# Loading the per-batch conditioning matrices by register-addressed transfers instead of gathers, with the first loads listed anew

## The chip, the cores and the metric

The kernel runs on one NeuronCore of one Trainium2 chip. A core has a matrix engine (TensorE, "PE" in the profile; its weight loads are "PEld"), a vector engine (VectorE, "DVE"), a scalar engine (ScalarE, "ACT"), a general engine (GpSimd, "POOL") and a queue engine (SyncE, "SP") which here only issues DMA transfers. ACT and POOL can issue transfers too. All engines run their own instruction lists in order and wait for each other by semaphores. The metric is the device time of one execution in microseconds (us); the kernel before has a median of 1348.92 us over 3 runs (1348.85 to 1357.19).

## The reference

```
y   = einsum('bct,bcd->bdt', x, cond_w[cond])      # x: (32, 64, 1024), cond_w: (16, 64, 64), cond: 32 integers
h   = gelu_tanh(y @ inter_w + inter_b)             # y as (32, 64, 1024); inter_w: (1024, 4096)
out = x + h @ output_w + output_b                  # output_w: (4096, 1024)
```

Everything is float32. Each of the 32 batches picks one of 16 matrices of 64 x 64 by its own index in `cond` and mixes its 64 channels by it. Then comes a feed-forward network over all 2048 rows (32 batches of 64), with a residual.

## The kernel before

**Mix.** The batches are taken in 16 pairs, since two batches of 64 channels fill 128 partitions. `load_x(i)` loads a pair of x (128 x 1024, 512 KB). `wsel(i)` is a 128 x 64 tile with the two matrices of the pair, one in each half of the partitions; `wsel_e` holds those of pairs 0 to 9, `wsel_l` those of pairs 10 to 15. `mix(i)` multiplies on TensorE with x as the stationary operand, so that y comes out transposed, into two PSUM tiles; `mixed(i)` copies these to SBUF, half by ACT, half by DVE. The tag that `mix` is given says which PSUM bank it uses (B, C, or a pool of its own); the feed-forward products use banks A, B and C too.

**Feed-forward.** Both matrix products are done by two levels of a Strassen-Winograd scheme: 7 products of blocks in place of 8, and each of the 7 by 7 smaller ones. The sums of blocks that this needs are made by POOL for the weights (`inner_w1`, `outer_w1`) and by DVE with copies by ACT for y (`right_sums`). The first product runs over 2 halves of the rows and 4 groups of hidden columns; `load_w1` loads a block of inter_w (1 MB; "11", "12", "21", "22" are its four quarters for one group; w11, w12 and so on below). Its PSUM results are called fA, fB and fC after their banks. After all of it the second product runs in the same way (zA, zB, zC), and the result is transposed and added to x.

**What sets the order.** The order is written out by hand. `at(time, fn, ...)` puts a step on a list with a time in units of one inner product (about 1.7 us); `run()` sorts the list and calls the steps in that order, and each engine executes its own instructions in the order of the calls. The numbers are thus only an order, not times on the chip.

**The opening.** Before: `start_rows` loads all of `cond`, broadcast to 128 partitions, by SP, and turns it into row numbers with an iota on POOL and two instructions on DVE. For pairs 0 and 1 (`NF = 2`) `first_rows` reads four indices into ACT's registers and issues four transfers of 16 KB from ACT, each addressed by a register. For the other fourteen pairs `gather` issues an indirect transfer from POOL, by the row numbers. `x` of pairs 2 and 3 and w11 are issued by ACT behind the four, all else by SP: x of 0, 1, 6, 7, then w12, w21, w22, then x of 4, 5, 8, 9. `x0` has six buffers, so that x of the seventh pair in the order waits for the first mix, and so on.

On PE the list is: `warm` (22 matmul passes on zeros), the mixes of pairs 0, 1 and 2, the first two inner products (fA, fB; they need w11 and the y of pairs 0 and 1), the mixes of pairs 3, 6, 7, 4, 5, 8 and 9, and then the third inner product (fC) and all others. Pairs 10 to 15 are mixed later, between the products.

Of the kernel before, what the change touches and what calls it, by code (L numbers as in the profile page):

```python
# [8 lines left out]

F32 = mybir.dt.float32  # L10
I32 = mybir.dt.int32
AF = mybir.ActivationFunctionType
ALU = mybir.AluOpType
PSUM = bass.MemoryType.PSUM
# [61 lines left out]
def kernel(  # L76
# [35 lines left out]
    nc = tc.nc  # L112
    P = 128
    B, C, T = x.shape
    S, _, D = cond_w.shape
    F = inter_w.shape[1]
    assert 2 * C == P and 2 * D == P
    NR = B // 2
# [3 lines left out]
    KQ = NK // 2  # L122
# [20 lines left out]
    x_rows = x.rearrange("(i j) c t -> i (j c) t", j=2)  # L143
    out_rows = out.rearrange("(i j) c t -> i (j c) t", j=2)
    w1_v = inter_w.rearrange("(k p) f -> p k f", p=P)
    w2_v = output_w.rearrange("(s A a u p) n -> a A s u p n", A=2, a=2, u=2, p=P)
    table = cond_w.rearrange("s c d -> (s c) d")


    const = ctx.enter_context(tc.tile_pool(name="const", bufs=1))  # L150
    NL = 6
    b1 = const.tile([P, F // P], F32, name="b1")
    rows = const.tile([P, NR], I32, name="rows")
    wsel_l = const.tile([P, NL, D], F32, name="wsel_l")
    wpool = ctx.enter_context(tc.tile_pool(name="w", bufs=6))
    cpool = ctx.enter_context(tc.tile_pool(name="c", bufs=14))
# [6 lines left out]
    x0 = right1.enter_context(ExitStack())  # L163
    xpool = x0.enter_context(tc.tile_pool(name="x0", bufs=6, side="right"))
    early = x0.enter_context(tc.tile_pool(name="early", bufs=1, side="right"))
    cond_sb = early.tile([P, B], I32, name="cond_sb")
    row_c = early.tile([P, NR], I32, name="row_c")
    wsel_e = early.tile([P, NR - NL, D], F32, name="wsel_e")
    pst = ctx.enter_context(tc.tile_pool(name="pst", bufs=2, space=PSUM))
    acc_pool = ctx.enter_context(tc.tile_pool(name="psacc", bufs=2, space=PSUM))  # L170
# [6 lines left out]
    def at(time, fn, *args):  # L177
        steps.append((time, len(steps), fn, args))
# [30 lines left out]
    def right_sums(time, get, gap=0.5):  # L209


        e = {}
        v = nc.vector

        def one():
            e.update(get())
            e["p"] = to_psum(e["12"])

        def two():
            add(v, e["t3"], e["22"], e["p"], sub=True)  # L220

        def three():
            add(v, e["t1"], e["p"], e["11"], sub=True)
            e["p"] = to_psum(e["11"])

        def four():
            add(v, e["t2"], e["p"], e["t3"])
            e["p"] = to_psum(e["21"])

        def five():  # L230
            add(v, e["t4"], e["p"], e["t2"], sub=True)

        for j, f in enumerate((one, two, three, four, five)):
            at(time + j * gap, f)
# [7 lines left out]
        return blk(q, b, a)  # L242


    def start_rows():
        nc.sync.dma_start(cond_sb, cond[None, :].to_broadcast([P, B]))
        cond_v = cond_sb.rearrange("p (i j) -> p j i", j=2)
        for j in range(2):
            half = slice(j * C, (j + 1) * C)
            nc.gpsimd.iota(row_c[half, :], [[0, NR]], channel_multiplier=1)  # L250
        for j in range(2):
            half = slice(j * C, (j + 1) * C)
            nc.vector.scalar_tensor_tensor(
                rows[half, :], cond_v[half, j, :], float(C), row_c[half, :],
                op0=ALU.mult, op1=ALU.add,
            )

    def wsel(i):
        return wsel_e[:, i, :] if i < NR - NL else wsel_l[:, i - (NR - NL), :]

    def gather(i):
        nc.gpsimd.indirect_dma_start(
            out=wsel(i),
            out_offset=None,
            in_=table,
            in_offset=bass.IndirectOffsetOnAxis(ap=rows[:, i : i + 1], axis=0),
        )

    def first_rows(n):

        _, idx = nc.values_load_multi_w_load_instructions(
            cond[None, : 2 * n], engines=[mybir.EngineType.Activation],
            min_val=0, max_val=S - 1,
            skip_runtime_bounds_check_because="the reference indexes cond_w by it",
        )
        for i in range(n):
            for j in range(2):
                nc.scalar.dma_start(
                    wsel(i)[j * C : (j + 1) * C, :],
                    cond_w[bass.ds(idx[2 * i + j], 1), :, :].rearrange("s c d -> (s c) d"),  # L280
                )


    XT = {}

    NF = 2
    FIRST = (0, 1, 2, 3, 6, 7, 4, 5)

    def load_x(i, eng=nc.sync):
        XT[i] = xpool.tile([P, T], F32, tag="x0", name=f"x0_{i}")  # L290
        eng.dma_start(XT[i], x_rows[i])

    def warm():

# [122 lines left out]
    def inner_y(a, p):  # L417
        q = Y[a, RIGHT[p]]
        pool = yia if p in (1, 2) else late["yib"]
        t = lambda n: pool.tile([P, 2, W], F32, tag=f"yi{p}", name=f"y{n}_{a}_{p}")  # L420
        t1 = blk(q, 0, 1)
        if (a, p) == (0, 1):
            t1 = cpool.tile([P, 2, W], F32, tag="c", name="yi1_0_1")
        YI[a, p] = {
            "11": blk(q, 0, 0),
            "21": blk(q, 1, 0),
            "22": blk(q, 1, 1),
            "12": blk(q, 0, 1),
            "t1": t1,
            "t2": t("i2"),  # L430
            "t3": t("i3"),
            "t4": t("i4"),
        }
        return YI[a, p]
# [1 line left out]

    W1 = {}

    def load_w1(it, n, eng=nc.sync):
        s = it % NG  # L440
        a, b = int(n[0]) - 1, int(n[1]) - 1
        t = wpool.tile([P, KQ, 4 * P], F32, tag="w", name=f"w{n}_{it}")
        eng.dma_start(t, w1_v[:, ts(b, KQ), ts(2 * s + a, 4 * P)])
        W1[it, n] = t

    def outer_w1(it, n):
# [238 lines left out]


    at(-61, warm)
    at(-60, start_rows)
    order = FIRST + (8, 9)
    at(-42, first_rows, NF)  # L690
    for j, i in enumerate(order[NF:] + tuple(range(NR - NL, NR))):
        at(-50 + 0.1 * j, gather, i)
    for n in Y_ORDER:
        at(-45, new_y, 0, n)
    MIX = 1.06
# [3 lines left out]
    for j, i in enumerate(order):  # L699
        t = M_AT[i]  # L700
        if j < 6:
            at(-43 if j < NF else -41 + 0.1 * j, load_x, i, nc.scalar if i in (2, 3) else nc.sync)
        else:
            at(M_AT[order[j - 6]] + MIX + 0.45, load_x, i)
        at(t, mix, i, {3: None}.get(j, "CBC"[j % 2 + (j > 3)]))
        at(t + MIX + 0.3, mixed, i)
    at(M_AT[9] + MIX + 1, store_y1, 8)
    at(-40.75, load_w1, 0, "11", nc.scalar)
    for j, n in enumerate(("12", "21", "22")):
        at(-39.4 + 0.01 * j, load_w1, 0, n)  # L710
    at(-1, lambda: nc.sync.dma_start(b1, inter_b.rearrange("(f p) -> p f", p=P)))
    at(M_AT[9] + MIX + 0.42, end_mix)
    right_sums(M_AT[3] + MIX + 0.5, lambda: inner_y(0, 1))
# [4 lines left out]
    right_sums(ty + 9.2, outer_y0(1, 0))  # L718
    for j, p in enumerate((6, 7, 4, 5, 3)):
        right_sums(7 * (j + 2) - (3.6 if p == 6 else 4.5), lambda p=p: inner_y(0, p))  # L720
    later = (12.5, 14.3, 21.8, 26.2, 33, 46.6)
    for j, t in enumerate(later):
        i = NR - NL + j
# [13 lines left out]
    for it in range(nit):  # L737
        a, s = divmod(it, NG)
        b0 = 49 * it
        if it > 0:  # L740
            for n, t in W_LOAD.items():
                at(b0 - 49 + t, load_w1, it, n)
        for n, t in W_AT.items():
            if it == 0:
                t = {1: -10, 2: -8, "s3": -6, "s1": -3}.get(n, t)
            if isinstance(n, str):
                at(b0 + t, outer_w1, it, n)
            else:
                at(b0 + t, inner_w1, it, n)
        for o, p in enumerate(OUTER):  # L750
            b = b0 + 7 * o
            plan_block(
                b, 1, 7 * it + o, (it, p), "f", mm1,
                lambda l, r, it=it, p=p, a=a: (w1_block(it, p, l), y_block(a, p, r)),
            )
            fin = STATE[p][1]
            if fin is not None:
                hidden(b, it, fin)
            if it == NG:
                at(b - 49 + 13, load_y1, Y_ORDER[o])  # L760
                right_sums(b - 49 + 20, lambda p=p: inner_y(1, p), gap=0.8)
        pieces = []
        if it == 1:
            for k in range(KQ):
                e = {}
                t = b0 + 5 + 10.8 * k
                at(t, load_piece, k, e)
                right_sums(t + 5, lambda k=k, e=e: piece_targets(k, e), gap=0.8)
                at(t + 10.5, store_piece, k, e)
        elif it >= 2:  # L770
            n = -(-len(w2_pieces) // (nit - 2))
            for j in range(n):
                i = (it - 2) * n + j
                if i < len(w2_pieces):
                    e = {}
                    t = b0 + 9.5 + 14 * j
                    pc = w2_pieces[i]
                    at(t - 6, load_w2, pc, e)
                    at(t - 2.5, early_t1, pc, e)
                    at(t + 0.6, store_w2, pc, e, ("11", "21", "22"))  # L780
                    right_sums(t, lambda pc=pc, e=e: w2_targets(pc, e), gap=0.8)
                    at(t + 5, store_w2, pc, e, ("t1", "t2", "t3", "t4"))
# [398 lines left out]
```

## Time and profile before

| | |
|---|---|
| median of 3 runs | 1348.92 us (1348.85 to 1357.19) |
| the profiled execution | 1348.21 us, of which span 1345.9 us from the first to the last instruction |
| PE, PEld busy | 1329.9 us (99%), 1165.1 us (87%) |
| DVE, ACT, POOL busy | 883.0 (66%), 487.5 (36%), 959.7 us (71%) |
| mean granted clock of PE | 0.997 |
| gathers on POOL | 14, of 0.94 to 1.10 us each, from 5.03 to 22.4 us |
| register-addressed transfers on ACT | 4, issued from 4.00 to 6.52 us |
| first mix, first fC | 8.35 us, 38.20 us |

All times inside the span count from its first instruction. "Busy" is the time in which an engine has an instruction of its own at work; a wait is written as who waited, for whom, how long in total, how often, and the longest. The last instruction that an engine waits for gets the whole wait.

### The profile page before, as it was taken

How to read it: one execution, taken by the hardware profiler on the slowest of the kernel's cores; microseconds unless marked ns; L12 is line 12 of the kernel's file. 1: busy time of each engine (PE TensorE's matmuls, PEld its weight loads, DVE VectorE, ACT ScalarE, POOL GpSimd, SP SyncE). 2: the span in 40 equal slices, each digit the busy share in tenths (PEclk: the TensorE clock that was granted, in tenths of full speed). 3: DMA queues.
4: the chain of work that ended last, by engine and by line, in shares of the span. 5: the costliest groups of instructions: out<-in, count | busy, mean ns of one | idle time of the engine just before them, and what ended most of it. 6: DMA issues, size and time to landing. Idle time of an engine off the chain costs nothing.

```text
span 1345.9 us, 18976 instructions
## 1 busy us (share of the span) xinstructions
PE 1329.9 (99%) x6542; PEld 1165.1 (87%) x6542; DVE 883.0 (66%) x1581; ACT 487.5 (36%) x985; POOL 959.7 (71%) x599
## 2 busy tenths in 40 slices
PE   8999999999999999999999999999999999999998
PEld 7888888888888888888888888888888888888887
DVE  3766566575787765757648574675766757767776
ACT  2524324243353442524515332333324333333341
POOL 7753756938768396594862967949959689496793
PEclk8999999999999999999999999999999999999999
DMA  8445677787897866758649145183360723916611
GB/s 298 141 159 211 215 213 253 242 274 240 299 354 230 284 214 217 265 196 272 238 177 339 38 162 229 48 306 132 102 274 7 294 99 110 359 40 232 253 47 63
DMA packets 135471, 273.39 MB, mean 203 GB/s; under 512 B 15728, under 2 KB 68208, under 8 KB 123728
## 3 DMA queue, kind: packets, MB, share of 16 engines
q1 hardware_dynamic: 133520, 269.43, 57.8%
q10 hardware_dynamic: 1408, 2.29, 0.5%
q8 instruction: 52, 0.85, 0.3%
q0 software_dynamic: 448, 0.46, 0.1%
q14 instruction: 43, 0.35, 0.1%
HBM read 167.28 MB, written 104.86 MB: 202 GB/s over the span
## 4 chain that ended last, share of the span: by engine, by line
PE 50%; POOL 2%; DVE 2%; DMA 2%; issue 1%; ACT 1%; SPq 0%; DVEq 0%; POOLq 0%; ACTq 0%
PE zA L555 22%; PE zC L555 11%; PE fA L544 6%; PE zB L555 6%; PE fC L544 3%; PE fB L544 1%; DMA out_dram<-xb 1%; POOL h L186 1%; DVE hs L186 1%; PE tp L1035 1%; DMA w2p<-in_L_ffn_output_w_dram 0%; ACT t L206 0%; POOL w2p L186 0%; POOL vt L186 0%; POOL ws L186 0%
## 5 line engine op out<-in xcount | busy, mean ns | idle before, releaser
L544 PE MATMUL fA<-yi,wi 128*128 128x256 f32 x896 | 212.9, 380 | 3.4 <-DVE fX L186 1.5
L186 DVE TENSOR_TENSOR hs<-h,t 128x512 f32<-128x512 f32 x308 | 200.3, 680 | 9.9 <-POOL h L186 5.9
L186 POOL TENSOR_TENSOR h<-h,h 128x1024 f32<-128x1024 f32 x84 | 196.2, 2366 | 2.9 <-DMA out_dram<-xb 2.3
L555 PE MATMUL zA<-hs,wt 128*128 128x256 f32 x840 | 197.9, 379 | 0.3 <-DVE mX L186 0.3
L544 PEld LDWEIGHTS fA<-yi,wi 128*128 128x128 f32 x896 | 169.2, 190 | 29.7 <-issue 2.9
L555 PEld LDWEIGHTS zA<-hs,wt 128*128 128x128 f32 x840 | 158.6, 190 | 21.6 <-issue 0.7
L569 ACT ACTIVATE fD<-fD,b 128x256 f32<-128x256 f32 x128 | 57.9, 500 | 184.4 <-DVE fD L186 179.9
L186 POOL TENSOR_TENSOR wi<-w 128x512 f32<-128x512 f32 x80 | 101.7, 1272 | 30.6 <-PE fC L544 23.2
L186 POOL TENSOR_TENSOR ws<-w,w 128x1024 f32<-128x1024 f32 x32 | 74.9, 2362 | 67.0 <-PE fA L544 47.5
L206 ACT COPY t<-h 128x512 f32<-128x512 f32 x140 | 81.8, 590 | 75.9 <-DVE hs L186 71.3
L206 ACT COPY t<-hs 128x512 f32<-128x512 f32 x112 | 65.4, 588 | 109.3 <-DVE hs L186 109.3
L186 POOL TENSOR_TENSOR wt<-v 128x512 f32<-128x512 f32 x35 | 44.7, 1277 | 81.6 <-DMA v<-w_d 77.7
L186 DVE TENSOR_TENSOR fX<-fA,fX 128x512 f32<-128x512 f32 x104 | 71.4, 686 | 44.5 <-PE fA L544 43.3
L186 POOL TENSOR_TENSOR wi<-w,wi 128x512 f32<-128x512 f32 x40 | 50.8, 1271 | 62.7 <-PE fA L544 56.1
L544 PE MATMUL fC<-y,wi 128*128 128x256 f32 x352 | 83.4, 380 | 0.1
L555 PE MATMUL zC<-hs,v 128*128 128x256 f32 x336 | 79.7, 380 | 0.8 <-DVE hs L186 0.8
L544 PE MATMUL fA<-yi,w 128*128 128x256 f32 x320 | 75.6, 379 | 0.0
L555 PE MATMUL zA<-h,wt 128*128 128x256 f32 x320 | 75.6, 379 | 0.0
L544 PEld LDWEIGHTS fC<-y,wi 128*128 128x128 f32 x352 | 66.8, 190 | 9.5 <-issue 0.5
L555 PEld LDWEIGHTS zC<-hs,v 128*128 128x128 f32 x336 | 63.7, 190 | 9.7 <-DVE hs L186 1.2
L544 PEld LDWEIGHTS fA<-yi,w 128*128 128x128 f32 x320 | 60.9, 190 | 8.2
L555 PEld LDWEIGHTS zA<-h,wt 128*128 128x128 f32 x320 | 60.7, 190 | 8.1
(185 smaller groups left out, 2797.1 us busy)
## 6 DMA issues: line engine op xcount, KB each, us to landing
h<-hs_d SPq DMA_DIRECT2D x56, 1024.0 KB, 5.5
w<-in_L_ffn_inter_w_dram SPq DMA_DIRECT2D x31, 1024.0 KB, 6.2
hs_d<-hs SPq DMA_DIRECT2D x96, 256.0 KB, 3.1
v<-w_d SPq DMA_DIRECT2D x21, 1024.0 KB, 9.2
hs_d<-fD SPq DMA_DIRECT2D x64, 256.0 KB, 3.2
w2p<-in_L_ffn_output_w_dram SPq DMA_DIRECT2D x32, 512.0 KB, 4.9
w_d<-w2p SPq DMA_DIRECT2D x64, 256.0 KB, 2.9
w_d<-w2t SPq DMA_DIRECT2D x48, 256.0 KB, 6.7
```

The source lines that it names most:

```text
L186: eng.tensor_tensor(o, a, b, ALU.subtract if sub else ALU.add)
L206: nc.scalar.copy(t, src)
L544: nc.tensor.matmul(acc[:, u, :], lt[:, k, ts(u, P)], rt[:, k, :], start=start and u == 0 and k == 0, stop=k == 1, skip_group_check=True,)
L555: nc.tensor.matmul(acc, wl[:, k, :], hr[:, k, :], start=start and k == 0, stop=k == NG - 1, skip_group_check=True,)
L569: nc.scalar.activation(t[:, u, :], t[:, u, :], AF.Gelu_apprx_tanh, bias=b1[:, f : f + 1])
L1035: nc.tensor.transpose(tp[:, v, ts(n0, P)], d[:, n0, ts(v, P)], late["ident"])
```

## The change

Every pair's two matrices now come by two transfers of 16 KB whose address is a register. `load_indices(i0)` reads eight indices (four pairs) into registers: those of pairs 0 to 3 on ACT, the others on SP, in three portions. `load_wsel(i)` issues the two transfers, on ACT for pairs 0 to 3 and on SP for all others. `start_rows`, `gather`, the row tiles and the table view are gone, and with them all of POOL's and DVE's part in this. All x and all w are issued by SP. The first loads on SP are listed as: x0, x1, indices of pairs 4 to 7, x2, w11, x3, x6, wsel 6, x7, wsel 7, wsel 4, wsel 5, x4, x5, w12, w21, w22, indices of pairs 8 to 11, wsel 8, wsel 9, x8, wsel 10, wsel 11, x9, inter_b, indices of pairs 12 to 15, wsel 12 to 15. The banks of the mixes after the fourth are exchanged, C for B, so that the tenth now uses B. POOL's first sums from w12 are listed slightly later (-7.5 in place of -8). The order on PE stays.

```diff
-    def start_rows():
-        nc.sync.dma_start(cond_sb, cond[None, :].to_broadcast([P, B]))
-        cond_v = cond_sb.rearrange("p (i j) -> p j i", j=2)
-        for j in range(2):
-            half = slice(j * C, (j + 1) * C)
-            nc.gpsimd.iota(row_c[half, :], [[0, NR]], channel_multiplier=1)
-        for j in range(2):
-            half = slice(j * C, (j + 1) * C)
-            nc.vector.scalar_tensor_tensor(
-                rows[half, :], cond_v[half, j, :], float(C), row_c[half, :],
-                op0=ALU.mult, op1=ALU.add,
-            )
-
...
-    def gather(i):
-        nc.gpsimd.indirect_dma_start(
-            out=wsel(i),
-            out_offset=None,
-            in_=table,
-            in_offset=bass.IndirectOffsetOnAxis(ap=rows[:, i : i + 1], axis=0),
-        )
-
-    def first_rows(n):
-
+    IDX = {}
+
+    def load_indices(i0):
+
+
+        eng = mybir.EngineType.SP if i0 else mybir.EngineType.Activation
         _, idx = nc.values_load_multi_w_load_instructions(
-            cond[None, : 2 * n], engines=[mybir.EngineType.Activation],
-            min_val=0, max_val=S - 1,
+            cond[None, 2 * i0 : 2 * i0 + 8], engines=[eng], min_val=0, max_val=S - 1,
             skip_runtime_bounds_check_because="the reference indexes cond_w by it",
         )
-        for i in range(n):
-            for j in range(2):
-                nc.scalar.dma_start(
-                    wsel(i)[j * C : (j + 1) * C, :],
-                    cond_w[bass.ds(idx[2 * i + j], 1), :, :].rearrange("s c d -> (s c) d"),
-                )
+        for k, v in enumerate(idx):
+            IDX[2 * i0 + k] = v
+
+    def load_wsel(i):
+        eng = nc.sync if i > 3 else nc.scalar
+        for j in range(2):
+            eng.dma_start(
+                wsel(i)[j * C : (j + 1) * C, :],
+                cond_w[bass.ds(IDX[2 * i + j], 1), :, :].rearrange("s c d -> (s c) d"),
+            )
...
-    at(-60, start_rows)
     order = FIRST + (8, 9)
-    at(-42, first_rows, NF)
-    for j, i in enumerate(order[NF:] + tuple(range(NR - NL, NR))):
-        at(-50 + 0.1 * j, gather, i)
+    at(-60, load_indices, 0)
+    for i in range(4):
+        at(-59, load_wsel, i)
+    at(-50, load_indices, 4)
...
         if j < 6:
-            at(-43 if j < NF else -41 + 0.1 * j, load_x, i, nc.scalar if i in (2, 3) else nc.sync)
+            at(-55 if j < 2 else -43 + 0.1 * j, load_x, i)
         else:
             at(M_AT[order[j - 6]] + MIX + 0.45, load_x, i)
-        at(t, mix, i, {3: None}.get(j, "CBC"[j % 2 + (j > 3)]))
+        if i > 3:
+            at(M_AT[1] + MIX + 0.6 if i > 7 else -43 + 0.1 * j, load_wsel, i)
+        at(t, mix, i, None if j == 3 else "CB"[j % 2])
         at(t + MIX + 0.3, mixed, i)
+    at(M_AT[1] + MIX + 0.55, load_indices, 8)
+    at(0, load_indices, 12)
     at(M_AT[9] + MIX + 1, store_y1, 8)
-    at(-40.75, load_w1, 0, "11", nc.scalar)
+    at(-42.75, load_w1, 0, "11")
     for j, n in enumerate(("12", "21", "22")):
-        at(-39.4 + 0.01 * j, load_w1, 0, n)
+        at(M_AT[order[1]] + MIX + 0.5 + 0.01 * j, load_w1, 0, n)
...
+    for j in range(NL):
+        at(M_AT[2] + MIX + 0.6 if j < 2 else 0.1 * j, load_wsel, NR - NL + j)
...
-                t = {1: -10, 2: -8, "s3": -6, "s1": -3}.get(n, t)
+                t = {1: -10, 2: -7.5, "s3": -6, "s1": -3}.get(n, t)
```

## The prediction

> **What bounds the kernel now.** I read the page first (busy shares and slices), then TensorE's waits, then the first 38 us by stage, then SP's queue. PE is busy nearly everywhere:
>
> ```profile
> PE 1329.9 (99%) x6542; PEld 1165.1 (87%) x6542; DVE 883.0 (66%) x1581; ACT 487.5 (36%) x985; POOL 959.7 (71%) x599
> PEclk8999999999999999999999999999999999999999
> ```
>
> The only slice with a reduced clock is the first of 33.6 us. The list of TensorE's waits over the whole span says where time can be won:
>
> ```profile
> PE fA L544 <- DMA w<-in_L_ffn_inter_w_dram: 3.9, 1, 3.9
> PE fA L544 <- DVE fX L186: 1.5, 4, 0.6
> PE fC L544 <- DVE ys L347: 0.9, 1, 0.9
> ```
>
> The first and the third lie in the opening that the diff rewrites; the rest is left alone. So the question is when the first fC (38.20 us) starts: from there PE runs densely to the end, and a shift there shifts the end one for one, as long as no other engine is short of slack. By stage (columns: window, length, busy us and count of PE, PEld, DVE, ACT, POOL, granted clock, DMA share, GB/s):
>
> ```profile
> 8.35:13.93 5.58, 5.57 (x97) 5.43 (x96) 1.51 (x4) 2.45 (x5) 4.06 (x6) 1.00 0.99 376
> 13.93:17.80 3.87, 0.00 (x0) 0.03 (x1) 0.76 (x2) 0.65 (x2) 2.96 (x4) 0.74 1.04 378
> 17.80:23.80 6.00, 6.00 (x16) 4.56 (x16) 0.00 (x0) 0.59 (x1) 4.94 (x6) 0.60 1.05 369
> 23.80:37.30 13.50, 13.49 (x225) 13.10 (x224) 10.64 (x23) 8.25 (x21) 13.27 (x9) 1.00 0.76 220
> ```
>
> Three mixes take 5.58 us (1.86 each). Then PE waits 3.87 us for w11. fA and fB follow at clock 0.60 in 6.0 us; later pairs take 1.89 + 1.73 = 3.6, so the pause costs 2.4 more. Seven mixes take 13.5 (1.93 each), and 0.9 goes to the evacuation of bank C. The DMA engines run flat out meanwhile:
>
> ```profile
> 5.70:9.00 3.30, 3.30 (x25) 2.71 (x23) 0.00 (x0) 0.78 (x1) 2.39 (x4) 1.00 0.63 222
> 9.00:31.50 22.50, 18.62 (x240) 16.96 (x237) 7.47 (x17) 7.27 (x19) 19.07 (x18) 0.85 1.04 378
> 31.50:34.00 2.50, 2.50 (x50) 2.50 (x47) 2.50 (x6) 1.45 (x4) 2.50 (x3) 1.00 0.83 20
> ```
>
> From 9 to 31.5 us they move 378 GB/s without a hole, and the mixes at the end follow arrivals by only 1 to 2 us. **DMA, not the index work, is the second bound of the opening**, so a hole in that stream matters. SP's own waits show what can make one:
>
> ```profile
> SPq L291 <- DMA wsel_e<-in_L_cond_weights_dram: 5.3, 1, 5.3
> SPq L291 <- DMA w<-in_L_ffn_inter_w_dram: 4.3, 1, 4.3
> SPq L291 <- DMA x<-in_x_dram: 1.0, 1, 1.0
> L271 ACTq TENSOR_LOAD <-in_itok_B_dram_ptr x1: 879/879/879, 0.7 to 0.7; - x1
> L271 ACTq TENSOR_LOAD <-in_itok_B_dram x1: 2185/2185/2185, 1.6 to 1.6; - x1
> ```
>
> An x load waits for a wsel, for w11 and for another x, to none of which it owes data. Listing the SP and ACT transfers in order (cond, x0, x1 and four wsel, x2, w11, x3, x6, x7, w12, w21, w22, x4, x5, x8, x9): x5 waits for w11, eight places earlier, and x8 for x3, eight earlier; x6 waits for a wsel at about that distance. So completion signals rotate over eight, and **a transfer is issued only when the one eight places before it has landed**. The change puts 32 small transfers into this rotation.
>
> **What the Trainium skill says.** "DMA: Bandwidth & Descriptors", Issuing engines are not separate DMA queues: transfers of SP, ACT and POOL share the same 16 engines, so another issuer saves only issue time. The 378 GB/s with three issuers agrees. The same page, Why a DMA increments its semaphore by 16 and not by 1: "One semaphore per in-flight slot, not one per stream"; the eight-back waits agree. "Runtime: NRT & Kernel Launch", Instruction fetch mechanics: a register load costs about 200 ns a register; here four took 2.19 us, so the trace is dearer. "TensorE: Matmul & The Clock Gate", Part 1: a window of about 3.4 us with PE idle halves the clock; here 3.87 us idle did so.
>
> **The change, part by part.**
>
> *Index loads.* Four registers take 2.19 us, two (the pointer) 0.88. Eight: at least 2.19 + 4 x 0.2 (skill) = 3.0, at most 2.19 + 4 x (2.19 - 0.88)/2 = 4.8. I take 4.2. On ACT: done at 1.64 + 4.2 = 5.85 instead of 3.83. On SP, behind x0 and x1 (issued by 1.6 now that cond_sb is gone): 0.9 + 4.2, so SP is blocked until 6.8. Behind it are queued all other loads. Two more such loads come later on SP.
>
> *wsel 0 to 3 on ACT.* The trace has 0.63 us per issue and 2.85 to land. wsel 0 is issued by 6.7 and lands at 9.55: mix 0 starts at 9.6, not 8.35. The eight issues end at 11.1; the table load (1.28) and mix 0's evacuation (1.17 from ACT's copy to DVE's end) are queued behind, so bank C is free at 13.6 and mix 2 runs 13.6 to 15.5 (before: to 13.93). Loss 1.6.
>
> *w11.* SP reaches it at 7.4, but its signal is then one of the first wsel (landing 8.9 to 9.6) or x1 (7.3). I take 8.9; a quiet 1 MB load (issued at 54.0) lands in 5.6, hence 14.5 (range 12.9 to 15.2). PE finds it: the 3.9 wait goes, and fA, fB run at full clock, 15.5 to 19.1, against 23.8.
>
> *Gathers, iotas, rows off POOL and DVE.* 14 gathers, 1.25 us apart, held POOL until 22.4; the inner sums of w11 (5.2 us) now follow w11 and are ready near 20. Worth nothing by itself: fC waited for DVE, not for these. Cover: the mixes up to fC.
>
> *The rest of SP's queue.* At 378 GB/s an x takes 1.39 us, a w 2.77. Behind w11 (14.5): x3 15.9, x6 17.3, x7 18.7, all ahead of need (19.1, 21.0, 22.9). The wsel of 6, 7, 4 and 5 are eight issues between these and x4; the eight-back waits bind: the first half of wsel 5 waits for x6 (17.3), x4 for wsel 6 and two issues (18.6), x5 for x7 (19.1). A lone x lands in 4.0 (xl): x4 at 22.6, x5 at 24.0, in time (needed 24.9, 26.8). That is a hole of about 2 us. Then w12, w21, w22 are streamed: 26.8, 29.6, 32.3. Issue of these, the third index load (0.9 + 4.2) and wsel 8, 9 (4 x 0.63) fit under that stream, to about 29. x8 stands in the ring behind w22: 32.3 + 0.2 + 1.4 = 33.9. wsel 11 waits for w22 (eight back): x9 is issued at 32.3 + 2 x 0.63 = 33.6 and lands at 37.6.
>
> *PE.* Five mixes end at 19.1 + 5 x 1.93 = 28.8. PE idles 5.1 us until x8; mix 9 runs 37.6 to 39.5. Bank tags: mix 9 is now in B, so fC need not wait for its evacuation (0.9 won). fC at 39.5 against 38.2: +1.3. The 5 us pause exceeds the 3.87 that halved the clock before; that cost 2.4, here mix 8 absorbs some of it under the wait for x9. I take 1.2, between 0 and 3.4. **Sum: +2.5 us.**
>
> *Behind fC.* w12 to w22 land by 32.3 against 28.0: POOL's sums from them shift by some 1 us at most, since the gathers no longer delay them; first used by PE near 60. The fourth index load and wsel 12 to 15 (5.1 + 8 x 0.63) push the first xl load from 39.2 to about 46.5, landing by 51; its mix is at 55.8. Both covered, the latter by 5 us.
>
> **Total.** Profiled execution 1348.2 (span 1345.9 and 2.3 around it) + 2.5 = 1350.7. It stands 0.7 under the median of the runs, so for that 1348.9 + 2.5 = **1351.4 us**.
>
> **The rivals.**
> A, the queue doesn't stall (not slower): w22 lands before 31.0, the point at which w22 + 1.3 + 4.0 + 1.9 gives fC at 38.2. Without holes, 7.4 MiB behind x0 and x1 at 378 GB/s are 20.5 us; from first bytes at 9.3 w22 lands at 29.8 with x8 and x9 close behind (32.6), mix 9 ends at 34.5: -3.7, 1345.2. For it: DMA held full rate for 22 us before. Against: SP then had only 17 transfers, now over 30 with waits eight back.
> B, x8 and x9 come in time as well, and PE's own sum holds: 15.5 + 3.6 + 13.5 = 32.6, -5.6, 1343.3. Needs x9 at 30.7, against 33.8 before; three w tiles stand ahead of it.
> C, the third index load is slow under full DMA (twice 4.2) and w22's issue blocks on a full ring, as SP's third w issue did for 3.3 us: x8 is issued near 36, x9 lands at 43, mix 9 ends at 45: +6.8, with the clock +8 to +10: near 1358.
> That the change doesn't do what it says: the gathers surely go; no case.
>
> **How the numbers follow.** Forecast 0.50 (1348.5 to 1354.5), A 0.20, B 0.08, C 0.22. The range from A's lower part to C's start, 1344 to 1357.5, leaves 2 in 10. Every case moves under 10 us of 1349, and 1% is 13.5, about what a measurement can tell from no change: same 0.96, faster 0.01, slower 0.03.
>
> **What would show it.** Right: no wait of fA for w; fA and fB in 3.6 us; two new TensorE waits of py for x or wsel between 28 and 38; a second low-clock stretch; TENSOR_LOAD near 4 us on SP; holes in DMA near 20 and 36. Wrong: x9 landing before 33, register loads near 3 us, or no waits on SP for wsel.

## The result, and the profile after

| | before | after |
|---|---|---|
| median of 14 runs each, same chip | 1349.87 us (1348.00 to 1357.19) | 1359.61 us (1355.49 to 1361.90) |
| the profiled execution, its span | 1348.21, 1345.9 us | 1359.90, 1357.8 us |
| first fC starts | 38.20 us | 43.45 us |

The ratio of the mean times, after to before, is 1.0053 (95% interval 1.0035 to 1.0071), so the change costs about 7 us, where 2.5 were forecast. The kernel before has a median near 1349 us on two chips (on which 6 of 14 and 8 of 26 executions took 1353 to 1358) and near 1358 on two others, the changed one about 1359 on both that it ran on. Every ratio below is therefore to the kernel before on the same chip. Traces are compared across chips too, where the landing of one and the same load can differ by 1 to 3 us.

The page of the changed kernel, PE's row of the busy times and its clock in 40 slices of 34 us:

```profile
PE 1335.2 (98%) x6542; PEld 1168.8 (86%) x6542; DVE 881.9 (65%) x1579; ACT 487.3 (36%) x985; POOL 946.1 (70%) x583
PEclk9799999999999999999999999999999999999999
```

POOL lost 13.6 us of busy time, but TensorE had no wait for POOL that this could end. PE became busier by 5.3 us with the same 6542 matmuls: they ran slower, and the second slice (34 to 68 us) shows where, at clock 0.7. TensorE's waits over the whole span:

```profile
PE py L302 <- DMA x<-in_x_dram: 9.3, 1, 9.3
PE zA L535 <- DVE mX L181: 2.0, 1, 2.0
PE fA L524 <- DVE fX L181: 1.5, 4, 0.6
```

The wait for w11 (3.9) and the one of fC (0.9) are gone. One of 9.3 us has come in, of mix 8 for x8, and a late one of 2.0 us. By stage (window, length, busy us and count of PE, PEld, DVE, ACT, POOL, clock, DMA share, GB/s):

```profile
7.81:14.10 6.29, 6.29 (x98) 6.11 (x97) 1.51 (x4) 2.68 (x6) 0.43 (x1) 1.00 0.90 308
14.10:17.75 3.65, 3.65 (x18) 2.96 (x17) 0.76 (x2) 1.13 (x3) 3.49 (x4) 1.00 0.89 315
17.75:27.10 9.35, 9.34 (x161) 9.20 (x160) 6.86 (x15) 5.27 (x13) 1.10 (x1) 1.00 0.85 302
27.10:36.34 9.24, 0.00 (x0) 0.03 (x1) 2.34 (x5) 1.66 (x4) 8.93 (x6) 0.57 0.65 230
36.34:43.45 7.11, 7.11 (x64) 7.00 (x64) 1.95 (x4) 1.16 (x4) 7.11 (x4) 0.50 0.63 82
43.45:49.66 6.21, 6.21 (x18) 5.03 (x18) 3.32 (x6) 2.21 (x5) 4.08 (x3) 0.57 0.32 100
```

Up to 27.1 us the change gains: fA and fB take 3.65 us at full clock, and mix 3 starts at 17.75 instead of 23.81, 6.1 us earlier. Then PE stands still for 9.24 us, the clock halves, mixes 8 and 9 take 7.11 us instead of 3.86, and fC with the product after it 6.21 instead of 3.53. The third product after fC, the first that is back in step, starts at 51.38 us, against 43.45 before: **+7.9 us from the opening**. This stays constant until 1289 us.

Why x8 is late is told by the chain of work that ended last, of the first 60 us of the changed kernel (start, length, what):

```profile
20.57 0.61 SPq L423
...
21.22 3.97 SPq L249
25.30 4.15 SPq L249
29.62 0.48 SPq L259
...
31.59 0.47 SPq L259
32.06 0.05 issue
32.16 4.10 DMA x<-in_x_dram
36.25 0.09 issue
36.34 7.18 PE py L302 x64
```

SP issues w22 (L423) at 20.57 and then stands in the third index load (L249) for 8.2 us, of which 3.97 are the pointer and 4.15 the eight registers. It issues the four halves of wsel 8 and 9 (L259), and x8 only at 32.16. The same loads, pointer (`_ptr`) and eight registers, take 3.6 us together on ACT at 0.7 us, and 3.5 on SP at 1.7 us (minimum, median and maximum in ns, then the first and last start):

```profile
L249 SPq TENSOR_LOAD <-in_itok_B_dram_ptr x3: 2615/3161/3970, 1.7 to 36.5; - x3
L249 SPq TENSOR_LOAD <-in_itok_B_dram x3: 914/1482/4152, 4.4 to 40.2; - x3
L249 ACTq TENSOR_LOAD <-in_itok_B_dram_ptr x1: 1030/1030/1030, 0.7 to 0.7; - x1
L249 ACTq TENSOR_LOAD <-in_itok_B_dram x1: 2534/2534/2534, 1.8 to 1.8; - x1
```

The remaining 4 us of the profiled execution are lost near its end: 11.9 us of span less 7.9. TensorE's order of work there, after and then before (start, busy us, what, idle before it and its releaser):

```profile
1300.46 1.89 PE L535 MATMUL zC<-h,vt 128*128 128x256 f32 x8
1304.39 3.22 PE L535 MATMUL zA<-hs,wt 128*128 128x256 f32 x8 [2.04 <-DVE mX L181]
1307.41 2.36 PE L535 MATMUL zA<-h,wt 128*128 128x256 f32 x8
```

```profile
1291.78 1.89 PE L555 MATMUL zC<-h,vt 128*128 128x256 f32 x8
1293.99 1.97 PE L555 MATMUL zA<-hs,wt 128*128 128x256 f32 x8 [0.32 <-DVE mX L186]
```

A pause of 2.04 us in place of 0.32, and then two products that take 3.0 and 2.2 us from start to start instead of 1.73: the clock halves once more. The two losses are the whole: from the third product after fC to the end, the four traces in which this pause occurs take 1305.4 to 1306.4 us, and the ten others of this document 1301.8 to 1302.9.

### The profile page after: what moved, and what is told of

Read it like the earlier page. It is cut to its first block, busy times and chain, and to the rows that moved or that the text cites. A ratio compares the mean times of both kernels' runs of the same rounds, so it can differ in the third digit from the quotient of the medians.

```text
span 1357.8 us, 19044 instructions
## 1 busy us (share of the span) xinstructions
PE 1335.2 (98%) x6542; PEld 1168.8 (86%) x6542; DVE 881.9 (65%) x1579; ACT 487.3 (36%) x985; POOL 946.1 (70%) x583
## 4 chain that ended last, share of the span: by engine, by line
PE 85%; DVE 5%; POOL 3%; issue 2%; ACT 2%; DMA 1%; SPq 1%; ACTq 1%; DVEq 0%; POOLq 0%
PE fA L524 25%; PE zA L535 23%; PE fC L524 12%; PE zC L535 11%; PE fB L524 6%; PE zB L535 6%; DVE hs L181 1%; PE py L302 1%; POOL h L181 1%; PE tp L1021 1%; ACT t L201 1%; DVE fX L181 1%; POOL w2p L181 1%; DMA x<-in_x_dram 1%; SPq L249 1%
## 5 line engine op out<-in xcount | busy, mean ns | idle before, releaser
L181 POOL TENSOR_TENSOR wi<-w,wi 128x512 f32<-128x512 f32 x40 | 50.9, 1271 | 63.4 <-PE fA L524 56.8
```

The source lines that it names most:

```text
L181: eng.tensor_tensor(o, a, b, ALU.subtract if sub else ALU.add)
```

## The experiments

Two theories stood against each other, with two side questions. **W**: x8 is late because 3 MB of w were listed ahead of it and because SP stands in the third index load; the halved clock then adds to it. Its rivals take one of these alone. The side questions were whether the gathers matter, and what the new order is worth without the new addressing. The first four kernels ran on one chip, on which the kernel before takes 1358.29 us (1356.93 to 1362.36); the changed kernel was not timed there.

### w12, w21, w22 behind x9 (e1)

```diff
-        at(M_AT[order[1]] + MIX + 0.5 + 0.01 * j, load_w1, 0, n)
+        at(M_AT[3] + MIX + 0.46 + 0.01 * j, load_w1, 0, n)
...
-                t = {1: -10, 2: -7.5, "s3": -6, "s1": -3}.get(n, t)
+                t = {1: -10, 2: -3.8, "s3": -3.7, "s1": -3}.get(n, t)
```

> The changed kernel with w12, w21 and w22 listed behind x9 on SP instead of ahead of x8 (POOL's sums from them follow in the list). Theory W (x8 comes late because 3 MB of w stand ahead of it in the ring and because the third register load holds SP for 8.3 us): with the 3 MB gone only the register load is left, 4 to 8 us from 20 on, then four wsel issues; x8 lands at 30 to 34 instead of 36.25, the pause of TensorE before mix 8 falls from 9.3 to 3 to 7 us, and the time falls by 3 to 8 us against the changed kernel. Rival R (the 32 small transfers on SP in the rotation of eight signals are what makes the loads late, wherever the w stand): x8 still lands at 35 or later, time unchanged within 2 us.

Measured: 1353.02 us (1350.20 to 1354.78), ratio 0.9955 (0.9941 to 0.9969) to the kernel before. The third index load took 2.53 + 0.90 us here; x8 was issued at 26.54 and landed at 30.47. TensorE:

```profile
30.60 6.98 PE L302 MATMUL py<-wsel_e,x 64*128 64x64 f32 x64 [2.89 <-DMA x<-in_x_dram]
37.52 3.78 PE L524 MATMUL fC<-yi,wi 128*128 128x256 f32 x8
```

The wait falls from 9.3 to 2.9 us, fC comes 5.9 us earlier than in the changed kernel. The order of w and x is worth most of the loss in the opening, in part because the index load, no longer beside the w tiles, is shorter (3.4 us instead of 8.2). The rival that the 32 small transfers make the loads late wherever the w stand had x8 at 35 or later, and is out in this form. The halved clock remains (mixes 8 and 9 take 6.9 us).

### No third index load (e2)

Pairs 8 to 11 take matrix 0, and the load of their indices is left out.

```diff
-                cond_w[bass.ds(IDX[2 * i + j], 1), :, :].rearrange("s c d -> (s c) d"),
+                cond_w[bass.ds(IDX[2 * i + j], 1) if 2 * i + j in IDX else slice(0, 1), :, :].rearrange("s c d -> (s c) d"),
...
-    at(M_AT[1] + MIX + 0.55, load_indices, 8)
```

> The changed kernel without the register load for pairs 8 to 11; these four pairs use matrix 0, by a fixed address, so that reading their indices is left out. Theory W as in the prediction: SP reaches x8 at about 24, but x8 stands behind w22 in the ring and lands near 34 (36.25 with the load): mix 8 starts 2.3 us earlier, the clock is still halved, the time falls by 1.5 to 4 us. If the register load alone is the cause (rival T), x8 lands before 29 and the pause is gone: the time falls by 11 us or more.

Measured: 1356.13 us (1353.73 to 1356.82), ratio 0.9979 (0.9969 to 0.9988). The chain of work that ended last, from 20 to 40 us:

```profile
27.20 9.19 DMA x<-in_x_dram
36.38 0.09 issue
36.48 3.03 PE py L302 x29
```

x8 is issued 5 us earlier than in the changed kernel and lands at the same time, 36.38: it is under way for 9.19 us instead of 4.10, behind w22, which lands at 34.93. Mix 8 was expected 2.3 us earlier and starts no earlier (36.48). The opening gains nothing (third product after fC at 51.06), and the late pause doesn't occur. So the index load alone isn't the cause; with the w ahead, x8 has two reasons to be late, and taking one away leaves the other. (PE's wait is only 2.9 us here because fA was late too, at 17.8 and half clock.)

### PE kept busy ahead of mix 8 (e3)

Twenty products on zeros are put in front of mix 8, into the tile that it overwrites.

```diff
+        if i == 8:
+            for _ in range(20):
+                nc.tensor.matmul(tiles[0][:, 1, :], Z["z"][:, :P], Z["z"][:, P:], start=True, stop=True)
```

> The changed kernel with 20 more matmuls of zeros on TensorE just ahead of mix 8, into the PSUM tile that mix 8 then overwrites: 8 to 9 us of work inside the pause of 9.3 us. Loads unchanged. If the halved clock after the pause costs about 5 us (two mixes of 3.6 us and two products of 3.8 and 2.8 us), it goes: mix 8 and 9 take 1.9 us each, but mix 9 then waits for x9 until 39.5; fC near 41.4 at full clock, the time falls by 4 us. If the slowness of the two mixes has another cause, nothing changes but for at most 1 us more.

Measured: 1356.53 us (1354.74 to 1360.48), ratio 0.9989 (0.9981 to 0.9997). TensorE:

```profile
29.86 8.90 PE L303 MATMUL py<-zeros 128*128 128x256 f32 x40
38.70 2.00 PE L307 MATMUL py<-wsel_e,x 64*128 64x64 f32 x32
40.88 2.12 PE L307 MATMUL py<-wsel_e,x 64*128 64x64 f32 x32 [0.18 <-issue]
42.93 1.99 PE L529 MATMUL fC<-yi,wi 128*128 128x256 f32 x8
```

From the start of mix 8 to the third product after fC (48.22) pass 9.5 us, against 15.0 in the changed kernel (36.34 to 51.38) and 13.6 in its repetition below (36.93 to 50.56). **The halved clock is worth 4.1 to 5.5 us.** Not all of it could be won in the changed kernel: at full clock mix 9 would have to wait for x9 (39.49, repeated 40.30) for 1.3 to 1.5 us, by estimate from these traces. x8 landed at 37.49 in this run and the products on zeros ended at 38.7, so that 1.2 us were given away too. The third product comes 2.3 to 3.2 us earlier than in the two traces of the changed kernel, where 4 us of time had been expected.

### The new order with the gathers (e4)

The kernel before, with x, w11 and w12 to w22 issued by SP in the order of the changed kernel, its bank tags, and its place for POOL's second sums:

```diff
-            at(-43 if j < NF else -41 + 0.1 * j, load_x, i, nc.scalar if i in (2, 3) else nc.sync)
+            at(-55 if j < 2 else -43 + 0.1 * j, load_x, i)
...
-    at(-40.75, load_w1, 0, "11", nc.scalar)
+    at(-42.75, load_w1, 0, "11")
...
-        at(-39.4 + 0.01 * j, load_w1, 0, n)
+        at(M_AT[order[1]] + MIX + 0.5 + 0.01 * j, load_w1, 0, n)
```

> The kernel before (gathers on POOL, two pairs by register on ACT) with the changed kernel's order of x and w on SP, and its PSUM banks. No register load and no wsel on SP. Theory W and R alike: SP issues x2 and w11 by 3 us, the stream has no hole, w11 lands by 11, x8 near 27 and x9 near 28 although the w stand ahead of them; mixes follow without pauses, fC near 31 to 33 at full clock: 5 to 7 us faster than the kernel before, 13 to 17 faster than the changed one. If the order of the w ahead of x8 is itself too much, TensorE waits for x8 for over 3 us here too and the time is at that of the kernel before or above.

Measured: 1357.58 us (1356.85 to 1359.62), ratio 0.9994 (0.9986 to 1.0002). The gain that was expected did not come. TensorE's waits of the first 60 us:

```profile
PE py L322 <- issue: 7.6, 8, 2.3
PE py L322 <- DMA wsel_e<-in_L_cond_weights_dram: 1.5, 2, 1.1
```

In mix 1 PE issues one to five matmuls at a time between 15 and 25 us, with pauses that no semaphore explains; fA starts at 29.4. This was not in any theory. It led to the question whether the kernel before does the same on such chips.

### The kernels before and after again, and both causes mended

These four (r1, r2, e8, e9) ran together on a second chip; the kernel before takes 1358.34 us there (1357.39 to 1360.70).

> The kernel before once more, for its trace on the chip of these runs. All theories: the trace agrees with the one shown (first mix near 8.4, mixes 1.9 each, fC near 38.2) if the chip's median is near 1349; if it is near 1358, as on the chip of the first four experiments, 8 to 9 us must be found in it. Theory S (TensorE's instruction supply is late when SP's stream fills the DMA engines early): the mixes of the opening then crawl, as in e4, with gaps that no semaphore explains, and fC starts 6 us or more later. Rival: the opening is unchanged and the loss lies late, in a pause of some 2 us and a clock window.

Measured: 1358.93 us, one run. TensorE's order of work, in which mix 1 has begun at 10.9 us:

```profile
17.05 0.99 PE L322 MATMUL py<-wsel_e,x 64*128 64x64 f32 x4 [1.43 <-issue]
19.22 0.44 PE L322 MATMUL py<-wsel_e,x 64*128 64x64 f32 x1 [1.18 <-issue]
...
22.02 0.46 PE L322 MATMUL py<-wsel_e,x 64*128 64x64 f32 x1 [1.85 <-issue]
...
28.01 3.41 PE L544 MATMUL fA<-y,w 128*128 128x256 f32 x8
```

It does: PE crawls from 12.8 to 24.8 us (8.1 us of such pauses in 10 waits), fA starts at 28.0 instead of 17.8 and fC at 47.46 instead of 38.20. By the third product after fC it is 10.9 us behind the trace first shown (54.40 against 43.45), of the 11.3 by which its span is longer: nearly all of the difference between these two executions lies in this opening.

> The changed kernel once more, on the same chip as e8 and e9. All theories: fC near 43.5, PE waits 9 us for x8, and 1358 to 1362 us; the median serves as base for e8 and e9.

Measured: 1358.71 us (1356.04 to 1360.83), ratio 1.0003 (0.9995 to 1.0011). The trace is that of the first chip: a wait of 9.9 us for x8, fC at 44.09, the late pause of 2.1 us. So on this chip the changed kernel's opening doesn't crawl in the trace taken, that of the kernel before does, and the two take the same time.

The third run moves w12 to w22 as above and, in addition, lets POOL load the indices and wsel of pairs 8 to 11:

```diff
-        eng = mybir.EngineType.SP if i0 else mybir.EngineType.Activation
+        eng = {0: mybir.EngineType.Activation, 8: mybir.EngineType.Pool}.get(i0, mybir.EngineType.SP)
...
-        eng = nc.sync if i > 3 else nc.scalar
+        eng = nc.scalar if i < 4 else nc.gpsimd if 7 < i < 12 else nc.sync
...
-    at(M_AT[1] + MIX + 0.55, load_indices, 8)
+    at(-50, load_indices, 8)
...
-            at(M_AT[1] + MIX + 0.6 if i > 7 else -43 + 0.1 * j, load_wsel, i)
+            at(-49 if i > 7 else -43 + 0.1 * j, load_wsel, i)
...
-        at(M_AT[2] + MIX + 0.6 if j < 2 else 0.1 * j, load_wsel, NR - NL + j)
+        at(-49 if j < 2 else 0.1 * j, load_wsel, NR - NL + j)
```

> The changed kernel with two edits: w12, w21, w22 are issued behind x9 (as in e1), and the indices and wsel of pairs 8 to 11 are loaded by POOL at the start, while POOL has nothing to do (before: until w11 lands at 13.6). Theory W (x8 is late because 3 MB of w stand ahead of it and because SP stands in the third register load): x8 is issued near 21 and lands near 25, x9 near 26.5, PE does not wait, no half clock after 13, fC near 31.0, against 37.5 in e1 and 43.5 in the changed kernel; 8 us under e1, 12 to 14 under the changed kernel. Rival (PE's half clock or the eight completion signals hold the mixes in any case): fC not before 35, gain over the changed kernel under 8.

Measured: 1345.56 us (1342.16 to 1346.56), ratio 0.9898 (0.9882 to 0.9913) to the kernel before, 13.2 us under the changed kernel. x8 landed at 26.66 and x9 at 30.00. TensorE:

```profile
17.34 3.77 PE L524 MATMUL fA<-y,w 128*128 128x256 f32 x8
...
22.77 13.50 PE L302 MATMUL py<-wsel_e,x 64*128 64x64 f32 x224
36.20 1.99 PE L524 MATMUL fC<-yi,wi 128*128 128x256 f32 x8
```

The seven mixes run without a wait in 13.50 us, as in the kernel before, and fC follows at full clock. fC was expected at 31.0 and came at 36.2: w11 landed 1.3 us later than in the changed kernel, mix 2 waited 0.66 us for a copy, and mix 2 and fA then ran at about half clock (0.53 and 0.50), so that fB ended at 22.77 instead of 17.7. The total came out in the expected range for another reason: 9.1 us are from the opening (third product after fC at 41.49 against 50.56), and 3.4 because the late pause is gone. The late start also makes it easier for x8: had five mixes ended at 27.1, as in the changed kernel, x8 would still have been in time, and x9 about 1 us late, by estimate from these landings.

> The changed kernel with the second edit of e8 alone: indices and wsel of pairs 8 to 11 come by POOL at the start, w12, w21, w22 stay ahead of x8. Theory W: x8 is issued before 24 (32.2 in the changed kernel), yet lands behind w22 near 33.7, x9 near 35; mix 8 starts near 33.7 instead of 36.3, half clock as before, fC near 40; 3 to 4 us under the changed kernel. Rival 1, the register load alone: x8 lands before 31, fC before 36, 7 us and more under. Rival 2, the w tiles alone: x8 lands at 36 as before, within 1 us of the changed kernel.

This is the second edit of the run before, alone. Measured: 1353.98 us (1352.76 to 1357.31), ratio 0.9968 (0.9956 to 0.9980), 4.7 us under the changed kernel. The chain of work that ended last, from 15 to 45 us:

```profile
22.76 12.53 DMA x<-in_x_dram
35.29 0.14 issue
35.43 7.18 PE py L302 x64
```

x8 is issued 10 us earlier and lands 1.6 earlier, after 12.53 us under way behind w22 (33.98). Of the 4.7 us only 1.4 are from the opening (third product at 49.20 against 50.56); the rest is the late pause, which is gone here too. The landing of x8 by the two causes:

| x8 lands, fC starts (us) | third index load on SP | not on SP |
|---|---|---|
| w12 to w22 ahead of x8 | 36.25, 43.45; repeated 36.84, 44.09; 37.49, 42.93 (PE kept busy) | 36.38, 44.21 (left out); 35.29, 42.54 (on POOL) |
| w12 to w22 behind x9 | 30.47, 37.52 | 26.66, 36.20 (on POOL) |

By pairs on the same chip, the w tiles cost 7.0 us of x8's landing with the index load on SP (30.47 against 37.49, which loads as the changed kernel does) and 8.6 without. The index load costs 1.1 us (left out) and 1.6 (on POOL) with the tiles ahead. With them behind it is 3.8, across two chips; part of this belongs to the wsel of pairs 8 and 9, which went to POOL as well and for which SP needs 2.4 us. The w tiles are thus the larger cause. Either is enough to make x8 later than 27.1, when the five mixes ahead of it end in the changed kernel.

### The part of the gathers

Does POOL's gathering make PE crawl? Three runs (r3, e10, e11) on a third chip, where the kernel before takes 1350.21 us (1347.33 to 1357.41):

> The kernel before a third time, for its trace on the chip of e10 and e11. All theories: if the median there is near 1358, the third mix crawls as in r1 (the PE waits for issue 8 us in all, fC near 47.5); if it is near 1349, the trace is the one first shown (fC near 38.2).

Measured: 1349.73 us, one run; fC at 39.84 after a wait of 5.5 us for w11, no crawl.

```diff
-        at(-50 + 0.1 * j, gather, i)
+        at(-50 + 0.1 * j if i < NR - NL else 4 + 0.1 * j, gather, i)
```

> The kernel before, with the gathers of pairs 10 to 15 put behind POOL's first sums, so that gathers run until about 14.9 us instead of 22.3. Theory G (while POOL gathers and the DMA engines are full, TensorE gets its instructions late, where the kernel before is slow): the crawl of the third mix ends some 2 us after the last early gather, near 17 instead of 25, fA starts near 19 instead of 28, and the time falls by 7 to 9 us, to about 1350. Rival (the gathers have no part in it, full DMA engines alone do it): mix 2 still ends near 28, within 2 us of the kernel before. Where the kernel before runs at 1349, both expect no crawl and no difference over 2 us.

Measured: 1348.39 us (1347.01 to 1354.82), ratio 0.9985 (0.9967 to 1.0004), no crawl. As the traced execution of the kernel before doesn't crawl on this chip, the run can't tell the two apart; the slower executions there (8 of 26 at 1354 to 1358 us, at a clock of 0.989 to 0.992, against 0.992 in r1) have no trace.

```diff
+    idle_g = early.tile([P, 13, D], F32, name="idle_g")
...
+    at(-60, start_rows)
     at(-60, load_indices, 0)
+    for i in range(2, NR - 1):
+        at(-50 + 0.1 * i, gather, i)
```

> The changed kernel, with thirteen gathers (and the load of cond, the iotas and the row numbers) put back on POOL at the start, into a tile that nobody reads. Theory G: TensorE crawls in mixes 1 or 2, its waits for issue sum up to 5 to 10 us before 25, fA starts after 20 instead of 14.1; part of that is hidden by the wait for x8, so the time rises by 1 to 6 us. Rival: no waits for issue, fA near 14.5 to 15.5, within 2 us of the changed kernel's 1358.7.

Measured: 1358.00 us (1355.71 to 1362.23), ratio 1.0051 (1.0035 to 1.0067). There are no waits for issue; POOL's first sum starts at 21.13 instead of 13.67, fA at 18.73 instead of 14.1 and fC at 45.6 instead of 43.5, yet the time is that of the changed kernel on the first chip (ratio 1.0053). In TensorE's waits from 8 to 50 us the one for x8 has shrunk by what fA lost:

```profile
PE py L328 <- DMA x<-in_x_dram: 4.7, 1, 4.7
```

The time agrees by luck: the third product after fC comes at 53.21, which is 1.8 and 2.7 us later than in the two traces of the changed kernel (on other chips), and the late pause, worth 4.0 in the first of them, is missing. So what was added may well cost something in the opening, most of it hidden by the wait for x8; on this evidence the removal of the gathers is neither worth nothing nor worth a known time. Whether they have a part in the crawl stays open: both traces that crawl have gathers (r1 and e4), but on this chip nothing crawled.

### Both causes mended, once more (e12)

> The kernel of e8 once more. Theory W (its gain over the changed kernel, 13 us on the chip of r2 and e8, comes from x8 and x9, so that it doesn't depend on how the kernel before runs): 1343 to 1347 again, wherever the kernel before stands; fC near 36, no wait of PE for x. Rival (the gain was the chip's): the time stands as far from the kernel before as there, near 1336 where the kernel before runs at 1349, or is back above 1349.

This ran on the second chip again, where the kernel before takes 1359.10 us this time. Measured: 1345.08 us (1341.31 to 1346.75), ratio 0.9887 (0.9867 to 0.9907). fC at 37.48, no wait for x. After a pause of 1.01 us in mix 0 the clock falls to half within 4 us and stays there up to fA:

```profile
9.97 8.12 PE L302 MATMUL py<-wsel_e,x 64*128 64x64 f32 x94 [1.01 <-DMA wsel_e<-in_L_cond_weights_dram]
18.03 3.78 PE L524 MATMUL fA<-y,w 128*128 128x256 f32 x8
```

So the gain repeats, but the rival that puts it down to the chip isn't tested. The kernel's 1345 us lie under every median of the kernel before; they were not measured beside one that runs at 1349.

## Why the prediction was right or wrong

The direction and its place were right: the opening, the wait of mix 8 and the halved clock. The size was not: the median lies 8.2 us above the forecast and 2.1 above the range's end; by the ratio the loss is 7.2 us, which would be 1356.1 on the time shown before, inside the range and above the 1348.5 to 1354.5 of the forecast itself.

| step | forecast | measured |
|---|---|---|
| mix 0 starts | 9.6 | 7.81 |
| w11 lands; fA; fB ends | 14.5; 15.5; 19.1 | 13.60; 14.10; 17.75 |
| five mixes end | 28.8 | 27.1 |
| w22 lands | 32.3 | 32.26 |
| third index load | 5.1 us | 8.2 us |
| x8, x9 land | 33.9, 37.6 | 36.25, 39.49 |
| fC starts | 39.5 (+1.3) | 43.45 (+5.3) |
| halved clock | +1.2 in all | 4.1 to 5.5 in all; +2.7 behind fC (repeated: +1.2) |
| late in the kernel | 0 | +4.0 |

*Right.* The wait for w11 goes, and fA and fB run in 3.65 us. The sum of the stream, with its rotating signals, gave w22's landing to 0.1 us, and this was no luck: the seven loads between w11 and w22 landed within 0.5 us of the forecast. SP waits for wsel before x and w, as forecast:

```profile
SPq L271 <- DMA wsel_e<-in_L_cond_weights_dram: 3.0, 2, 1.8
SPq L423 <- DMA wsel_e<-in_L_cond_weights_dram: 2.1, 1, 2.1
```

The wait of fC for bank C is gone, as the exchange of banks was to bring about: it is 0.9 us in the four traces with the old tags and in none of the ten with the new ones. That the gathers are worth nothing is not shown: the run that adds them to the changed kernel has the same time, but a later opening.

*Wrong, first: "Issue of these, the third index load (0.9 + 4.2) and wsel 8, 9 fit under that stream, to about 29".* The eight registers were sized right (4.15), the pointer was not: the 0.9 us were read from a load at 0.7 us into the kernel, when the DMA engines were still idle, and under load it took 3.97. That alone moved x8's issue from about 29 to 32.16, as late as w22's landing, so that nothing of its 4.1 us was covered: x8 landed 4.0 us behind w22, where 1.6 were forecast. The rule for a covered x8 was right, for it landed 1.3 and 1.5 us behind w22 in the two runs that keep the w tiles ahead and have no third index load on SP. Only w22 itself came later there (33.98 and 34.93), as it did in the run with PE kept busy (33.63), which has that load. Rival C had named the slow index load (8.4 us); its second half, an issue of w22 that blocks on a full ring, didn't occur, as the three w were issued between 19.55 and 21.18 without a pause.

*Wrong, second: "two new TensorE waits" and the price of the clock, "I take 1.2".* There is one wait: mix 8 at half clock lasts until x9 is there. The price was taken from the pause of 3.87 us in the kernel before, where full products followed; here 64 small matmuls follow, and it is 4.1 to 5.5 us by the run in which PE is kept busy. Of the 4.0 us by which fC is later than forecast, 1.9 are x9's and 2.0 the halved clock in the mixes; another 2.7 come behind fC, 1.2 in the repetition.

*Wrong, third: nothing was expected behind the opening.* The late pause occurs in four traces (the changed kernel's two, w behind x9, PE kept busy) and not in the other kernels', whose openings are both earlier and later; so the shift isn't its cause. In the changed kernel POOL's sum of h near 1271 us waits 4.5 us for DVE's mX, against 2.3 for a transfer in the kernel before; in the four traces this wait is 3.6 to 5.1 us, in the ten others 1.7 to 2.8. The four are just the kernels in which SP makes the third index load and POOL issues no transfer. What sets the wait off was not tried, and stays open.

## What to carry to other kernels

A register load holds its whole queue, and its price under a full DMA stream can be more than twice that at the start of the kernel (8.2 us against 3.5): put it on an engine that has nothing to do yet. In a stream that runs at full rate the order is the arrival; what PE needs first must stand ahead of the large tiles, and a transfer with two reasons to be late may gain little when only one of them is taken away (1.1 to 1.6 us here for the index load alone). Price a pause of PE by what follows until the clock is back, not by the pause.

## What the runs showed of the hardware

**A register load by SP is dearer under a full DMA stream.** The same pointer took 0.9 to 1.0 us on ACT or POOL at the start, 2.5 to 2.6 on SP beside some 300 GB/s (the first load, and the third in e1), and 3.6 to 5.5 beside 380 to 401 GB/s; the eight registers took 0.9 to 4.2. The rate isn't the whole of it, as the pointer of the fourth load took 3.2 to 3.5 beside some 110 GB/s. "DMA: Bandwidth & Descriptors", Latency and other measured facts, in the Trainium skill gives 0.2 us on average and 2 us at high load for one access to HBM; the pointer's 3.97 and 5.37 us exceed that, so the measurement decides here.

**The mixes don't bring the clock back.** In the kernel before seven mixes of 64-wide tiles hold a full clock for 13.5 us. But after a pause, PE was busy with two mixes for 7 us at 0.50 and stayed there; the full clock came back 2.4 to 5.4 us after the start of the first full product (fC), in the changed kernel, its repetition, e1, e2, e9 and e11 (worked out as twice the time by which fC and the product after it exceed the 3.53 us of the kernel before). "TensorE: Matmul & The Clock Gate", Part 1, lets one busy window of about 3.4 us suffice; that agrees for the products, not for these mixes.

**A short pause can halve the clock, or not.** The prediction went by a pause of 3.87 us. In six traces (e2, e3, e8, e9, e11, e12) a pause of only 0.66 to 1.14 us within the first three mixes was followed by a fall to half clock within these mixes; where they had no pause (before, after, r2, e1, r3, e10) they held 1.00. But 0.88 us ahead of fC did nothing in three traces (before, r3, e10) and was followed by 0.58 in r1, and of the four late pauses of 2.0 us three halved the clock and the repetition's did not. The length of a pause alone doesn't decide.

**PE can crawl with no wait in sight**: 8 us in 10 pauses in mixes 1 and 2 of the kernel before in one trace, and none in two others, on other chips. Its cause is open.
